# A graph attention layer on one core: the last stage in units of 500 nodes between the last steps, first indices loaded early, target products ten quads behind

## The chip, the cores and the metric

The kernel runs on one core of a Trainium2 chip. The metric is the device time of one execution in microseconds (us). Five engines work side by side, each through its own list of instructions: PE (matrix products), DVE (VectorE), ACT (ScalarE), POOL (GpSimd) and SP (SyncE, which here only issues transfers). Transfers between DRAM and the on-chip memory are issued by SP, ACT or POOL and carried out by 16 DMA engines of the core. An instruction waits on semaphores, and what stands behind it on its engine waits with it.

## The reference, cut to what matters

There are N = 12,500 nodes with 128 channels and E = 400,000 edges, sorted by their target `dst`. The targets are not spread evenly: they are drawn as 12,500 times the square of a uniform number, so many edges go to low nodes.

```python
h = relu(layernorm(x))
message = (h @ w_src + b_src)[src] + (h @ w_dst)[dst]
message = message * edge_weight * radial_mlp(edge_attr)     # three layers, 32-64-64-128
message = message @ w_sep + b_sep                           # 8 heads: 16 alpha, 16 value channels
score = einsum(leaky(alpha), alpha_dot)                     # one for each edge and head
att = segment_softmax(score, dst)
out = x + segment_sum(value * att, dst) @ w_proj + b_proj
```

## The kernel before, in words

**Node stage (L157 to L436).** A loop runs over 25 quads (four tiles of 128 nodes). For quad i it turns and normalizes, makes the source product `products(i, 0)` (L272, stored into the DRAM table `t_src` at L288), and the target product of four quads earlier, `products(i - 4, 1)`, for `t_dst`. After the loop come the last four target products and `cuts()` (L364 to L400), which makes the score vectors on PE (L372) and stores the list `same`, which marks where the target changes. In turn i = 6 `first()` loads the first 128 x 128 source indices `ri` (L295) and turns them into the index tile `idx0` that the first gathers need (L297 to L301). `fits()` (L309) counts sections whose targets span too many nodes into `bad`; if it is not zero, another path runs (it doesn't with these inputs).

**Steps.** The edges form 782 sections of 512, and two sections make a step: NP = 391 steps. `step(k)` (L1219) is a software pipeline written out by hand: in one step it issues loads for later edges (SP: weights, targets, `md` rows of `t_dst` at L844), gathers the source rows for step k + 2 (POOL, L865, an indirect transfer of 128 rows each, 3125 in all), makes messages and scores for steps around k, and LAG = 13 steps later weighs the values and sums them by target in windows of W = 64 nodes: `ob` (L1080). `store_win` (L1084) stores a step's windows into `win`, and `store` (L1087, L1088) writes the 63 first rows of each of the two windows into the DRAM table `agg` (numerator and denominator for each node), at a row number that SP reads from memory. The rows of `agg` are set to zero in the first ten steps by 20 transfers of 125 rows (`zero`, L139). Order and queue of every instruction are those of the program.

**Blocks.** A window's last node can be shared with the next window. Thirteen blocks of 64 sections join these border rows: `block_load`, `block_rows` (loads `rr` from `win`, L1134), `block_maxima`, `block_factors`, `block_columns` (L1163, L1166), `block_totals`, `block_out` into DRAM `obs_d`, and `scatter` (L1195), an indirect transfer on POOL that puts a block's 128 rows into `agg`.

**Drain (L1356 to L1365).** After the last gather, 14 more steps (j = 0 to 13) finish the windows still in the pipeline. In between stand the jobs of the last two blocks, and in steps j = 2 to 12 one load of a finished block's rows (`comb`, L1362) and one scatter. Eight loads on ACT's queue (L1385) bring x + b_proj (`xb`, written earlier) into one tile `x_fin`. A window store into `agg` and a scatter into it are ordered by the program's tracking of dependencies, except in groups that are declared free of each other.

**Last stage (L1390 to L1448).** After the last block's scatter, ten loads bring all of `agg` (`g`, L1399; partition p holds nodes 97p to 97p + 96). Twelve tiles at a time, DVE divides numerator by denominator (L1409 to L1411); for each quad PE turns the quotients (L1422), ACT copies them (L1425), PE multiplies by w_proj (L1433), DVE adds `x_fin` (L1436) and SP stores `out` (L1437).

Of the kernel before, what the change touches and what calls it, by code (L numbers as in the profile page):

```python
# [32 lines left out]
H = 8  # L33
# [23 lines left out]
def gnn_kernel(ctx: ExitStack, tc: tile.TileContext, a: dict, out: bass.AP):  # L57
# [9 lines left out]
    NX = -(-NP // MP) * MP * PR  # L67
    assert NT * P == E and RC * RP == E and NT % TPI == 0 and NT % SORT_T == 0
# [88 lines left out]
    with tc.tile_pool(name="node", bufs=2) as np_, tc.tile_pool(name="node1", bufs=1) as n1, \  # L157
# [22 lines left out]
        ends = n1.tile([NH, 17, 2], I32, name="ends")  # L180
        eb = n1.tile([P, NS, 2], I32, name="eb")
# [6 lines left out]
        def load_targets():  # L188

            nc.sync.dma_start(out=cur[:, 1:CC + 1], in_=dst.rearrange("(p c) -> p c", p=P))  # L190
            at = dst[CC - 1:CC]
            with nc.allow_non_contiguous_dma(reason="single targets"):
                nc.sync.dma_start(out=cur[1:P, 0:1], in_=bass.AP(at.tensor, at.offset, [[CC, P - 1], [1, 1]]))
                at = dst[0:1]
# [97 lines left out]
        def first():  # L292

            ri = n1.tile([P, P], I32, name="ri")
            nc.sync.dma_start(out=ri, in_=src.rearrange("(t p) -> t p", p=P)[0:P, :])  # L295
            rows_0 = n1.tile([P, P], F32, name="rows_0")
            nc.vector.tensor_copy(rows_0, ri)  # L297
            pt = nps.tile([P, P], F32, name="tot", bufs=1)
            nc.tensor.transpose(pt, rows_0, ident)
            nc.vector.tensor_copy(idx0, pt)  # L300
# [8 lines left out]
        def fits():  # L309
# [14 lines left out]
            nc.vector.tensor_copy(bad, sum_)  # L324
# [85 lines left out]
        for i in range(Q):  # L410
# [4 lines left out]
            if i >= 4:  # L415
                products(i - 4, 1)
# [17 lines left out]
        for i in range(Q - 4, Q):  # L434
            products(i, 1)
        cuts()  # L436
# [313 lines left out]
    def windows():  # L750
# [7 lines left out]
        with tc.tile_pool(name="ps", bufs=1, space=PSUM) as pp, \  # L758
# [326 lines left out]

            def store(c, f):
                at = nc.sync.value_load(base[0:1, f, c:c + 1])  # L1087
                st = nc.sync.dma_start(out=agg[ds(at, W - 1), :], in_=accs[c][f * W:(f + 1) * W - 1, :])  # L1088
                if 2 * c + 1 >= (NC - 1) * (P // 2):
                    tc.declare_no_dep(st.ins, group="combined", reason="its rows follow those of the blocks")  # L1090
# [102 lines left out]
            def scatter(g):  # L1193
# [6 lines left out]
                tc.add_to_no_dep_group("combined", st.ins)  # L1200

            comb = {}

            def combined(g):
                comb[g] = tail_pool.tile([P, ROW], F32, name="comb", bufs=2)
                return comb[g]
# [12 lines left out]
            def step(k):  # L1219
# [63 lines left out]
                if has(c - 1):  # L1283
                    sums(c - 1)
                    if k >= NP:
                        store_win(c - 1)
                        store(c - 1, 0)
                        store(c - 1, 1)
# [40 lines left out]

            for k in range(-5, NP):  # L1330
                step(k)
            held.close()


            tail_pool = held.enter_context(tc.tile_pool(name="fin1", bufs=1, side="right"))
            x_fin = tail_pool.tile([P, NB, C], F32, name="x_fin")
            x_loads = load_xb(x_fin)
            last = NC - 1

            def out_rows(g):  # L1340
                block_rows_out(g, combined(g))
                scatter(g)

# [9 lines left out]
                10: lambda: out_rows(last - 1),  # L1353
            }
            assert SB * (NC - 1) + LAG + 1 == NP + 7
            for k in range(NP, NP + LAG + 1):  # L1356
# [9 lines left out]
            for _ in x_loads:  # L1366
                pass
            block_rows(last)
# [4 lines left out]
            with tc.tile_pool(name="fin", bufs=3) as fp:  # L1373
                final(fp, x_fin, lambda i: pp.tile([P, 4, P], F32, name=("pm0", "pm1", "V")[i % 3]),
                      lambda i: pp.tile([P, 4, C], F32, name=("p3", "pa", "m1")[i % 3]))


    XQ = 12
    out_v = out[0:NF * P, :].rearrange("(p t) c -> p t c", t=NF)
    agg_v = agg[0:NF * P, :].rearrange("(p t) c -> p t c", t=NF)  # L1380

    def load_xb(x_fin):

        for t0, t1 in groups:
            nc.scalar.dma_start(out=x_fin[:, t0:t1, :], in_=xb_v[:, t0:t1, :])  # L1385
            yield
        nc.scalar.dma_start(out=x_fin[:tail, NF, :], in_=xb[NF * P:N, :])
        yield

    def final(fp, x_fin, turned, product):  # L1390
        starts = list(range(0, NB, XQ))
        gs, qs, qTs = {}, {}, {}

        def load_g(i):

            gs[i] = fp.tile([P, XQ, ROW], F32, name="g", bufs=len(starts))
            for n, t0, t1 in blocks(starts[i], min(starts[i] + XQ, NB)):
                o = starts[i]
                nc.sync.dma_start(out=gs[i][:n, t0 - o:t1 - o, :],  # L1399
                                  in_=agg_v[:, t0:t1, :] if n == P else agg[NF * P:N, :].unsqueeze(1))  # L1400

        def quotients(i):
            r = fp.tile([P, XQ, H], F32, name="r")
            qs[i] = fp.tile([P, XQ, C], F32, name="q")
            g = gs.pop(i)
            for n, t0, t1 in blocks(starts[i], min(starts[i] + XQ, NB)):
                s = slice(t0 - starts[i], t1 - starts[i])
                m = t1 - t0
                nc.vector.tensor_scalar(r[:n, s, :], g[:n, s, C:ROW], 1e-16, None, op0=ALU.add)  # L1409
                nc.vector.reciprocal(r[:n, s, :], r[:n, s, :])  # L1410
                nc.vector.tensor_mul(  # L1411
                    qs[i][:n, s, :].rearrange("p t (h k) -> p (t h) k", h=H),
                    g[:n, s, 0:C].rearrange("p t (h k) -> p t h k", h=H),
                    r[:n, s, :].unsqueeze(3).to_broadcast([n, m, H, C // H]))

        def turn(i):
            t0, t1 = quads[i]
            q, o = qs[t0 // XQ], t0 // XQ * XQ
            pt = turned(i)
            for t in range(t0, t1):  # L1420
                n = rows(t)
                nc.tensor.transpose(pt[:, t - t0, :n], q[:n, t - o, :], ident[:n, :n])  # L1422
            w = (t1 - t0 - 1) * P + rows(t1 - 1)
            qTs[i] = fp.tile([P, 4, P], F32, name="qT")
            nc.scalar.copy(qTs[i].rearrange("p u n -> p (u n)")[:, :w], pt.rearrange("p u n -> p (u n)")[:, :w])  # L1425

        def finish(i):
            t0, t1 = quads[i]
            qT = qTs.pop(i)
            py = product(i)  # L1430
            for t in range(t0, t1):
                n = rows(t)
                nc.tensor.matmul(py[:n, t - t0, :], qT[:, t - t0, :n], w_proj, start=True, stop=True)  # L1433
            for n, u0, u1 in blocks(t0, t1):
                y = x_fin[:n, u0:u1, :]
                nc.vector.tensor_add(y, py[:n, u0 - t0:u1 - t0, :], y)  # L1436
                nc.sync.dma_start(out=out_v[:, u0:u1, :] if n == P else out[NF * P:N, :].unsqueeze(1), in_=y)  # L1437

        for i in range(len(starts)):
            load_g(i)  # L1440
        quotients(0)
        turn(0)
        for i in range(Q):
            if i % 3 == 1 and i // 3 + 1 < len(starts):
                quotients(i // 3 + 1)
            if i + 1 < Q:
                turn(i + 1)
            finish(i)  # L1448

# [4 lines left out]
    with fit.Else():  # L1454
# [23 lines left out]
        with tc.tile_pool(name="fin_b", bufs=3) as fp, tc.tile_pool(name="fin1_b", bufs=1) as f1, \  # L1478
                tc.tile_pool(name="fin_ps", bufs=2, space=PSUM) as fps, tc.manual_schedule():
            x_fin = f1.tile([P, NB, C], F32, name="x_fin")  # L1480
            for _ in load_xb(x_fin):
                pass
            final(fp, x_fin, lambda i: fps.tile([P, 4, P], F32, name="pt"),
                  lambda i: fps.tile([P, 4, C], F32, name="py"))
# [36 lines left out]
```

## Time and profile before

| | |
|---|---|
| time, median of 3 runs | 4215.05 us (4213.84 to 4223.81) |
| the profiled execution | 4210.53 us, of which the span from first to last instruction is 4208.8 us |
| mean granted clock of PE | 0.977 of full |
| first and last gather start | 82.7 and 4012.2 us |
| PE, DVE, ACT, POOL busy | 93%, 74%, 45%, 72% of the span |
| moved by DMA | 783 MB, 186 GB/s in the mean |

All times within the execution count from the span's start. A row of a timeline gives start and length in us, the engine (a "q" behind it marks an instruction of its sequencer, such as the issue of a transfer), the line, the operation, the tiles as out<-in, and how many instructions were merged; brackets hold the idle time ahead and what ended it. A row of the waits gives who waited for what: us in total, times, longest.

### The profile page before, as it was taken

What the parts mean: (1) busy time and instruction counts of PE and PEld (TensorE: products, weight loads), DVE (VectorE), ACT (ScalarE), POOL (GpSimd) and SP (SyncE); (2) the same over time, 40 slices, a digit from 0 to 9 for tenths busy, and PEclk for the clock granted to TensorE, in tenths of its full rate; (3) what the DMA queues carried; (4) which work ended last, traced back from release to release, by engine and by line L of the source; (5) the groups of instructions that cost most, each with busy time, mean ns of one, the idle gap of its engine ahead of it and who ended that gap; (6) DMA issues with size and microseconds to landing.
All of it is one profiled execution on the core that took longest, in us unless ns stands there. A gap on an engine that the chain in (4) does not pass through costs nothing. (4 is left out here: it accounts for less than half of the span.)

```text
span 4208.8 us, 87885 instructions
## 1 busy us (share of the span) xinstructions
PE 3913.5 (93%) x29351; PEld 2388.5 (57%) x29351; DVE 3104.8 (74%) x6187; ACT 1901.2 (45%) x4549; POOL 3010.2 (72%) x3195
## 2 busy tenths in 40 slices
PE   6889999999999999999999999999999999999975
PEld 5345555555555555555555555555555555555554
DVE  5567777777777777777777777777777777777754
ACT  5344444444444444444444444444444444444421
POOL 4777777777777777777777777777777777777710
PEclk8899999999999999999999999999999999999988
DMA  6767776777776776777777776676677776766634
GB/s 238 235 181 183 187 193 178 197 192 180 198 193 178 197 194 185 189 197 190 184 192 192 181 194 185 177 188 183 178 187 187 185 183 181 189 179 182 184 86 161
DMA packets 593333, 783.08 MB, mean 186 GB/s; under 512 B 125553, under 2 KB 392302, under 8 KB 592740
## 3 DMA queue, kind: packets, MB, share of 16 engines
q1 hardware_dynamic: 384786, 514.16, 40.6%
q0 software_dynamic: 100416, 205.44, 23.9%
q10 hardware_dynamic: 107666, 57.76, 4.7%
q8 instruction: 234, 3.83, 0.4%
q14 instruction: 231, 1.89, 0.1%
HBM read 637.83 MB, written 139.30 MB: 185 GB/s over the span
## 5 line engine op out<-in xcount | busy, mean ns | idle before, releaser
L865 POOL DMA_INDIRECT gs<-t_src,idx x3125 | 2972.3, 951 | 969.2 <-issue 807.5
L954 ACT ACTIVATE sl<-pa,c_b_a 128x512 f32<-128x512 f32 x782 | 536.9, 687 | 1018.6 <-PE pa L952 1009.9
L959 DVE SCALAR_TENSOR_TENSOR al<-pa,sl 128x512 f32<-128x512 f32 x782 | 540.5, 691 | 594.3 <-ACT sl L954 582.9
L1063 PEld LDWEIGHTS V<-c_w_v,mT 128*128 128x128 f32 x6048 | 746.8, 194 | 292.3 <-DVE ob L1080 119.1
L1063 PE MATMUL V<-c_w_v,mT 128*128 128x128 f32 x6048 | 879.4, 289 | 0.0
L952 PE MATMUL pa<-mT,c_w_a 128*128 128x512 f32 x1564 | 814.0, 603 | 3.9 <-DVE mT L946 3.6
L1065 DVE TENSOR_TENSOR pvx<-V,Pem 128x512 f32<-128x512 f32 x756 | 519.2, 687 | 243.4 <-PE V L1063 230.3
L932 PEld LDWEIGHTS pm<-ident,gs 128*128 128x128 f32 x3125 | 393.3, 142 | 420.4 <-issue 289.6
L1076 PEld LDWEIGHTS misc<-pvx,oh 128*64 128x64 f32 x6250 | 352.5, 137 | 410.6 <-ACT h L888 394.3
L924 DVE SCALAR_TENSOR_TENSOR rad<-p,c_fc_b,w_b 128x512 f32<-128x512 f32 x782 | 550.3, 745 | 39.4 <-PE p L916 3.7
L1076 PE MATMUL misc<-pvx,oh 128*64 128x136 f32 x6250 | 453.8, 287 | 118.3 <-ACT h L888 108.3
L946 DVE SCALAR_TENSOR_TENSOR mT<-pm,c_b_src,rad 128x512 f32<-128x512 f32 x782 | 550.7, 746 | 4.8 <-PE pm L939 4.8
L902 ACT ACTIVATE h<-p,b 128x512 f32<-128x512 f32 x391 | 287.5, 735 | 419.8 <-PE p L899 369.1
L932 PE MATMUL pm<-ident,gs 128*128 128x128 f32 x3125 | 471.9, 274 | 0.0
L916 PE MATMUL p<-h,w3b 64*128 64x512 f32 x1564 | 405.4, 595 | 11.5 <-ACT h L902 11.5
L939 PE MATMUL pm<-ohT,m 64*128 64x512 bf16 x2346 | 323.3, 382 | 0.0
L985 ACT ACTIVATE Sp<-m,b_s 128x512 f32<-128x512 f32 x192 | 131.9, 687 | 394.2 <-PE m L968 394.2
L884 PE MATMUL m<-eT,w1b 64*128 64x256 f32 x782 | 274.4, 431 | 26.1 <-DVE M L1006 16.7
L884 PE MATMUL misc<-eT,w1b 64*128 64x256 f32 x782 | 274.4, 431 | 0.0
L1049 DVE TENSOR_TENSOR oh<-lane,misc 128x504 f32<-128x504 f32 x391 | 262.3, 671 | 0.0
L899 PE MATMUL p<-h,w2b 64*64 64x256 f32 x3128 | 259.8, 403 | 0.0
L952 PEld LDWEIGHTS pa<-mT,c_w_a 128*128 128x128 f32 x1564 | 241.9, 195 | 21.2 <-DVE mT L946 8.1
(172 smaller groups left out, 3649.1 us busy)
## 6 DMA issues: line engine op xcount, KB each, us to landing
w_b<-in_edge_weight SPq DMA_DIRECT2D x390, 512.0 KB
d_b<-in_dst SPq DMA_DIRECT2D x390, 256.0 KB
gs<-t_src,idx POOLq DMA_INDIRECT x3125
e_t<-in_edge_attr ACTq DMA_DIRECT2D x390, 128.0 KB
sc_d<-Sp SPq DMA_DIRECT2D x192, 256.0 KB
win<-ob SPq DMA_DIRECT2D x391, 68.0 KB
agg<-ob SPq DMA_DIRECT2D x782, 33.5 KB
md<-t_dst SPq DMA_DIRECT2D x782, 32.0 KB
```

The costliest lines, as they stand in the source:

```text
L865: nc.gpsimd.indirect_dma_start(out=gs[:, t, :], out_offset=None, in_=t_src[:, :], in_offset=bass.IndirectOffsetOnAxis(ap=idx[:, t0 + t:t0 ...
L884: nc.tensor.matmul(p1[q], w1b[s, :], eTs[k][s, :], start=True, stop=True)
L916: nc.tensor.matmul(p3s[k][:, f, 0:SEC], w3b[s, :], h2s[k][s, :], start=True, stop=True)
L924: nc.vector.scalar_tensor_tensor(rad[:, s], p3[:, f, 0:n], b3, w_g[k][:, s], op0=ALU.add, op1=ALU.mult)
L932: nc.tensor.matmul(pms[k, f][:, t * T:(t + 1) * T], gs[:, t, :], ident, start=(t == 0), stop=False, is_transpose=True, skip_group_check=True)
L946: nc.vector.scalar_tensor_tensor(mTs[k][:, s], pms.pop((k, f))[:, 0:n], b_n, rad[:, s], op0=ALU.add, op1=ALU.mult)
L952: nc.tensor.matmul(pa[:, 0:n], w_a, mTs[k][:, f * SEC:f * SEC + n], start=True, stop=True)
L954: nc.scalar.activation(sl[:, 0:n], pa[:, 0:n], AF.Silu, bias=b_a, scale=1.0)
L959: nc.vector.scalar_tensor_tensor(al, pa, 0.25, sl, op0=ALU.mult, op1=ALU.add)
L1063: nc.tensor.matmul(V[:, t, :], mTs[c][:, o:o + T], w_v, start=True, stop=True)
L1065: nc.vector.tensor_mul(pvx[c][:, f, 0:n, 0:C].rearrange("p t (h k) -> p t h k", h=H), V[:, 0:n, :].rearrange("p t (h k) -> p t h k", h=H), ...
L1076: nc.tensor.matmul(acc[f * W:(f + 1) * W, :], ohs[c][:, f * TS + t, :], pvx[c][:, f, t, :], start=(t == 0), stop=(t == n - 1), skip_group_ ...
```

## The change

- `ri` is loaded on SP right behind the first group of x, not in turn 6. Two more single targets (`lim`) are loaded and four small DVE operations add to `bad` whether they are as high as the units below need.
- Target products run ten quads behind the source products instead of four; `cuts()` comes after `products(19, 1)`, so five target products stand behind it.
- The rows of blocks 0 to 10 are brought by four loads in steps NP - 6 to NP - 3, and all eleven scatters are issued at the end of step NP - 3, behind the last gather.
- New groups (`order`) declare that window stores and scatters of different sections are free of each other, and that loads of low nodes need only early sections.
- The last block's rows come in two parts (`last_rows`, `last_rows_2`), the last two of each window straight from the on-chip tile.
- The last stage works in 25 units of 500 nodes, 125 partitions with four nodes each. Seven loads of `g` (ACT's queue) and three of x (SP) are issued in step j = 0; from j = 2 on, `run` finishes one or two units in every step. Units 23 and 24 are loaded on SP after the last scatter.

```diff
         for t0, t1 in groups:
             nc.sync.dma_start(out=x_all[:, t0:t1, :], in_=x_v[:, t0:t1, :])
+            if t0 == 0:
+                ri = n1.tile([P, P], I32, name="ri")
+                nc.sync.dma_start(out=ri, in_=src.rearrange("(t p) -> t p", p=P)[0:P, :])
...
-            if i >= 4:
-                products(i - 4, 1)
+            if i >= 10:
+                products(i - 10, 1)
             products(i, 0)
...
-        for i in range(Q - 4, Q):
+        for i in range(Q - 10, Q):
             products(i, 1)
-        cuts()
+            if i == Q - 6:
+                cuts()
...
                 st = nc.sync.dma_start(out=agg[ds(at, W - 1), :], in_=accs[c][f * W:(f + 1) * W - 1, :])
-                if 2 * c + 1 >= (NC - 1) * (P // 2):
-                    tc.declare_no_dep(st.ins, group="combined", reason="its rows follow those of the blocks")
+                order(st.ins, 2 * c)
...
             for k in range(-5, NP):
                 step(k)
+                if 0 <= k - (NP - 6) < 4:
+                    bring(k - (NP - 6))
+                if k == NP - 3:
+                    for g in range(NC - 2):
+                        scatter(g)
...
-                if 0 <= j - 2 < NC - 2:
-                    nc.sync.dma_start(out=combined(j - 2), in_=obs_d[(j - 2) * P:(j - 1) * P, :])
-                    scatter(j - 2)
-                if j >= 3:
-                    next(x_loads, None)
+                if j == 0:
+                    un.load_x(0, 3)
+                    for u in range(7):
+                        un.load_g(u)
+                if j == 1:
+                    un.quotients(0)
+                    un.quotients(1)
+                    un.turn(0)
+                if j >= 2:
+                    un.run(1 + j % 2, EARLY)
+            un.run(1, EARLY)
             block_columns(last)
+            un.run(1, EARLY)
             block_totals(last)
             out_rows(last)
+            un.run(NU, EARLY)
             work.close()
+            un.run(NU, NU)
...
+    UP, UT = 125, 4
+    UN = UP * UT
...
+        def view(self, t, u):
+            return t[u * UN:(u + 1) * UN, :].rearrange("(p t) c -> p t c", t=UT)
+
+        def load_x(self, u0, u1):
+            for u in range(u0, min(u1, NU)):
+                self.x[u] = self.pool.tile([UP, UT, C], F32, name="xu", bufs=self.nx)
+                nc.sync.dma_start(out=self.x[u], in_=self.view(xb, u))
+
+        def load_g(self, u):
+            self.g[u] = self.pool.tile([UP, UT, ROW], F32, name="g", bufs=self.ng)
+            eng = nc.scalar if u < EARLY else nc.sync
+            self.ng_ = u + 1
+            ld = eng.dma_start(out=self.g[u], in_=self.view(agg, u))
...
+        def finish(self, u):
+            qT, py, y = self.qT.pop(u), self.product(u), self.x.pop(u)
+            for t in range(UT):
+                nc.tensor.matmul(py[:UP, t, :], qT[:, t, :], w_proj, start=True, stop=True)
+            nc.vector.tensor_add(y, py[:UP], y)
+            nc.sync.dma_start(out=self.view(out, u), in_=y)
+            self.nf = u + 1
+
+        def run(self, n, end):
+            for _ in range(n):
+                if self.nf >= end:
+                    return
+                u = self.nf
+                while self.ng_ < min(u + 8, end):
+                    self.load_g(self.ng_)
+                while self.nq < min(u + 3, end):
+                    self.quotients(self.nq)
+                while self.nt < min(u + 2, end):
+                    self.turn(self.nt)
+                self.finish(u)
+                self.load_x(u + 3, u + 4)
```

More of the change, by code (lines that the diff above doesn't have):

```diff
@@ L67, in gnn_kernel @@
     NX = -(-NP // MP) * MP * PR
+    NU = 25
+    EARLY_1, EARLY = 20, 23
+    EARLY_S = [(-(-2 * NS // P) - i) * (P // 2) for i in (2, 1)]
     assert NT * P == E and RC * RP == E and NT % TPI == 0 and NT % SORT_T == 0
@@ L180, in gnn_kernel @@
         ends = n1.tile([NH, 17, 2], I32, name="ends")
+        lim = n1.tile([1, 2], I32, name="lim")
         eb = n1.tile([P, NS, 2], I32, name="eb")
@@ L193, in load_targets @@
                 nc.sync.dma_start(out=cur[1:P, 0:1], in_=bass.AP(at.tensor, at.offset, [[CC, P - 1], [1, 1]]))
+                for i, s in enumerate(EARLY_S):
+                    nc.sync.dma_start(out=lim[:, i:i + 1], in_=dst[s * SEC:s * SEC + 1].unsqueeze(1))
                 at = dst[0:1]
@@ L323, in fits @@
             nc.vector.tensor_reduce(sum_, tot, AX.X, ALU.add)
-            nc.vector.tensor_copy(bad, sum_)
+            low = n1.tile([1, 2], F32, name="low")
+            for i, u in enumerate((EARLY_1, EARLY)):
+                nc.vector.tensor_scalar(low[:, i:i + 1], lim[:, i:i + 1], float(u * (N // NU)), None, op0=ALU.is_lt)
+            nc.vector.tensor_add(sum_, low[:, 0:1], sum_)
+            nc.vector.tensor_add(bad, low[:, 1:2], sum_)
             nc.sync.dma_start(out=ends_d[:, 1:2 * NS + 1].rearrange("o (p c) -> (o p) c", p=NH),
@@ L1084, in store_win, with order @@
                 nc.sync.dma_start(out=win[c * P:(c + 1) * P, :], in_=accs[c])
+            def order(ins, s, whole=False):
+                i = 1 if s < EARLY_S[0] else 2 if s < EARLY_S[1] else 3
+                for j in (1, 2):
+                    if j < i:
+                        tc.declare_no_dep(ins, group=f"early_{j}", reason="its rows follow those of the earlier sections")
+                    if i <= j:
+                        tc.declare_no_dep(ins, group=f"later_{j}", reason="its rows precede those of the later sections")
+                if whole and i < 3:
+                    tc.add_to_no_dep_group(f"early_{i}", ins)
+                if i > 1:
+                    tc.add_to_no_dep_group(f"later_{i - 1}", ins)
             def store(c, f):
@@ L1200, in scatter @@
                 tc.add_to_no_dep_group("combined", st.ins)
+                order(st.ins, g * (P // 2), True)
             comb = {}
-            def combined(g):
-                comb[g] = tail_pool.tile([P, ROW], F32, name="comb", bufs=2)
-                return comb[g]
             stages = {0: lambda g: (block_load(g), block_rows(g)), 2: block_maxima, 4: block_factors,
@@ L1328, in step, with bring, last_rows, last_rows_2 @@
                     stages[o](j)
+            def bring(j):
+                g0, g1 = 3 * j, min(3 * j + 3, NC - 2)
+                t = lp.tile([P, 3, ROW], F32, name="e_t", bufs=4)
+                nc.sync.dma_start(out=t[:, 0:g1 - g0, :],
+                                  in_=obs_d[g0 * P:g1 * P, :].rearrange("(g p) c -> p g c", p=P))
+                for g in range(g0, g1):
+                    comb[g] = t[:, g - g0, :]
+            assert NC - 2 <= 12
             for k in range(-5, NP):
                 step(k)
+                if 0 <= k - (NP - 6) < 4:
[3 more added lines that the diff above has]
+                        scatter(g)
             held.close()
-            tail_pool = held.enter_context(tc.tile_pool(name="fin1", bufs=1, side="right"))
-            x_fin = tail_pool.tile([P, NB, C], F32, name="x_fin")
-            x_loads = load_xb(x_fin)
+            fin = held.enter_context(tc.tile_pool(name="fin", bufs=2, side="right"))
             last = NC - 1
+            un = Units(fin, 8, 9, lambda u: pp.tile([P, 4, P], F32, name=("V", "pa")[u % 2]),
+                       lambda u: pp.tile([P, 4, C], F32, name=("p3", "m1")[u % 2]))
             def out_rows(g):
-                block_rows_out(g, combined(g))
+                comb[g] = fin.tile([P, ROW], F32, name="comb")
+                block_rows_out(g, comb[g])
                 scatter(g)
+            def last_rows():
+                q, s = width(last) // 2, last * (P // 2)
+                rrs[last] = sp.tile([P, ROW], F32, name="rr", bufs=1)
+                for i in range(2):
+                    nc.sync.dma_start(out=rrs[last][i * q:(i + 1) * q - 2, :],
+                                      in_=rows_w[s:s + q - 2, i * (W - 1), :])
+            def last_rows_2():
+                q = width(last) // 2
+                for i in range(2):
+                    nc.sync.dma_start(out=rrs[last][(i + 1) * q - 2:(i + 1) * q, :],
+                                      in_=accs[NP - 1][i * (W - 1):i * (W - 1) + W + 1:W, :])
             jobs = {
@@ L1378, in gnn_kernel @@
[L1378 to L1448, printed above, removed]
@@ new lines, in windows, with __init__, quotients, turn @@
+            un.run(NU, NU)
+    UP, UT = 125, 4
+    UN = UP * UT
+    assert N % UN == 0 and NU == N // UN
+    class Units:
+        def __init__(self, pool, nx, ng, turned, product):
+            self.pool, self.nx, self.ng, self.turned, self.product = pool, nx, ng, turned, product
+            self.x, self.g, self.qT = {}, {}, {}
+            self.nq = self.nt = self.nf = self.ng_ = 0
+        def view(self, t, u):
[9 more added lines that the diff above has]
+            ld = eng.dma_start(out=self.g[u], in_=self.view(agg, u))
+            if u < EARLY_1:
+                tc.declare_no_dep(ld.ins, group="later_1", reason="their nodes follow those of the early units")
+            if u < EARLY:
+                tc.declare_no_dep(ld.ins, group="later_2", reason="their nodes follow those of the early units")
+                tc.add_to_no_dep_group("early_1" if u < EARLY_1 else "early_2", ld.ins)
+        def quotients(self, u):
+            g = self.g[u]
+            r = self.pool.tile([UP, UT, H], F32, name="r")
+            nc.vector.tensor_scalar(r, g[:, :, C:ROW], 1e-16, None, op0=ALU.add)
+            nc.vector.reciprocal(r, r)
+            q = g[:, :, 0:C].rearrange("p t (h k) -> p t h k", h=H)
+            nc.vector.tensor_mul(q, q, r.unsqueeze(3).to_broadcast([UP, UT, H, C // H]))
+            self.nq = u + 1
+        def turn(self, u):
+            g, pt = self.g.pop(u), self.turned(u)
+            for t in range(UT):
+                nc.tensor.transpose(pt[:, t, :UP], g[:, t, 0:C], ident[:UP, :UP])
+            self.qT[u] = self.pool.tile([P, UT, UP], F32, name="qT")
+            nc.scalar.copy(self.qT[u], pt[:, :, :UP])
+            self.nt = u + 1
+        def finish(self, u):
+            qT, py, y = self.qT.pop(u), self.product(u), self.x.pop(u)
+            for t in range(UT):
+                nc.tensor.matmul(py[:UP, t, :], qT[:, t, :], w_proj, start=True, stop=True)
[15 more added lines that the diff above has]
+                self.load_x(u + 3, u + 4)
@@ L1477, in gnn_kernel @@
               ea_s.rearrange("(t p) c -> p t c", p=P), "b")
[L1478 to L1484, printed above, removed]
+        with tc.tile_pool(name="fin_b", bufs=3) as fp, tc.tile_pool(name="fin_ps", bufs=2, space=PSUM) as fps, \
+                tc.manual_schedule():
+            un = Units(fp, 10, 10, lambda u: fps.tile([P, 4, P], F32, name="pt"),
+                       lambda u: fps.tile([P, 4, C], F32, name="py"))
+            un.load_x(0, 3)
+            un.run(NU, NU)
 def kernel(**inputs):
```

14 lines of the change are left out of this document (5 added, 9 removed).

## The prediction, made before the changed kernel was run

> **What bounds the kernel now.** I read the page first (busy shares), then the times of all gathers, then the stretches of 20 us at the end, and last the queues' own waits. Columns of a timeline row: start, length, engine ("SPq" is an instruction that issues or waits), line, operation, tiles, count, and in brackets the idle time before it and what ended it.
>
> ```profile
> PE 3913.5 (93%) x29351; PEld 2388.5 (57%) x29351; DVE 3104.8 (74%) x6187; ACT 1901.2 (45%) x4549; POOL 3010.2 (72%) x3195
> L865 POOL DMA_INDIRECT gs<-t_src,idx x3125: 940/944/2243, 82.7 to 4012.2; - x196
> 82.70:482.70 400.00, 298.95 (x313) 0.91 0.70 192
> 882.70:1282.70 400.00, 302.74 (x320) 0.99 0.73 191
> ```
>
> PE is 93% busy, yet POOL sets the pace: 320 gathers in 400 us are one every 1.25 us, and 3125 of them fill 82.7 to 4012.2 nearly without a hole. An earlier first gather moves the rest with it. What lies outside the gathers is 82.7 us ahead and 4208.8 - 4013 = 196 us behind, and both ends are changed.
>
> The front, in which the change moves a load and six products:
>
> ```profile
> 35.44 0.23 DVE L297 CAST rows<-ri 128x128 f32<-128x128 int32 x1 [7.93 <-DMA ri<-in_src]
> 35.72 0.48 PE L299 MATMUL tot<-ident,rows 128*128 128x128 f32 x1 [8.73 <-DVE rows L297]
> 76.01 6.44 PE L272 MATMUL pm<-w_nodes,x_all 128*128 128x128 f32 x56
> 82.29 0.39 PE L372 MATMUL pt<-c_w_proj,bvb 128*128 128x128 f32 x2
> 98.74 0.27 SPq L398 DMA_DIRECT2D same<-more  x1
> 100.63 1.23 SPq L844 DMA_DIRECT2D md<-t_dst  x2
> ```
>
> DVE and PE stand 8 to 9 us for the first indices; after the products PE makes the score vectors (L372), and only at 98.74 is the last of `same` stored and at 100.63 the first `md` brought, which the first steps need.
>
> The end:
>
> ```profile
> 4040.00:4060.00 20.00, 17.00 (x145) 12.15 (x144) 13.02 (x29) 6.25 (x16) 0.00 (x0) 1.00 0.13 32
> 4060.00:4080.00 20.00, 11.32 (x110) 9.85 (x111) 8.27 (x20) 2.09 (x10) 1.02 (x1) 0.93 0.62 203
> 4140.00:4160.00 20.00, 10.19 (x64) 9.60 (x64) 9.94 (x13) 3.51 (x6) 0.00 (x0) 0.69 0.99 388
> SPq L1088 <- DMA agg<-comb,ids: 20.5, 4, 11.0
> SPq L1088 <- DMA agg<-ob: 12.8, 14, 3.6
> 4126.51 0.30 DVE L1080 TENSOR_TENSOR ob<-misc,bare 128x136 f32<-128x136 f32 x1 [1.10 <-PE misc L1076]
> 4139.32 6.87 SPq L1399 DMA_DIRECT2D g<-agg  x10
> ```
>
> The stretches give busy PE, PEld, DVE, ACT, POOL, PE's clock, the share of the 16 DMA engines and GB/s. In 4040 to 4060 PE works 17 of 20 us. Then the window stores wait for the scatters (20.5 us in four waits between 4050 and 4140), PE falls to 11, and the DMA engines are mostly free. From the last window's sums (4126.51) 12.8 us pass to the loads of `g`; then 128-row loads run at 388 GB/s with all 16 engines busy (0.99), 388 / (0.99 x 16) = 24.5 GB/s for one engine.
>
> **The change, part by part.**
>
> *Front.* With `ri` in SP's line behind the first x group the 8.7 us stall goes. Six more quads of target products stand behind the last source product: 48 matmuls at 6.44 / 56 = 0.115 us, 5.5 us, of which I count 2 to 3, since DVE and ACT must keep the pace too. So the gathers could start about 11 us earlier. But the first steps need `md`, and that stands behind the cuts, `same` and now four more stores of t_dst; it gains the stall less those stores. I take **7 us** off the whole, between 3 and 11. The two loads of `lim` and the four tiny DVE operations lie beside the x loads; cost nothing, at most 1 us.
>
> *Scatters.* Eleven scatters go out in a row after the last gather (POOL is idle there: 0.00 in 4040 to 4060), with their rows brought by four loads in place of eleven. The 20.5 us of waits go. What is late next is not PE but the units, as follows.
>
> *The units.* Each of the 25 units moves 125 rows of 2,048 bytes in (x), 125 of 2,176 in (g) and 125 of 2,048 out: 784,000 bytes, 19.6 MB in all. Before, these transfers had 128 rows. The question is what a transfer of 125 rows gets, and one such stands in the trace: the zeros of `agg`, 125 rows of 2,720 bytes.
>
> ```profile
> agg<-z SPq DMA_DIRECT2D x20, 332.0 KB
> 209.82 3.37 SPq L139 DMA_DIRECT2D agg<-z  x2
> 214.37 0.36 SPq L986 DMA_DIRECT2D sc_d<-Sp  x1
> SPq L991 <- DMA sc_d<-Sp: 9.1, 1, 9.1
> ```
>
> Two of them are issued by 213.2. The 256 KB store of `sc_d` behind them keeps SP waiting 9.1 us (its next issue is at 223.93), while PE, DVE and ACT stand. The DMA view of 218 to 223, inside that wait, in 40 slices of 0.125 us (busy tenths, then GB/s), and its queue rows (q1 is SP's, q0 POOL's gathers):
>
> ```profile
> DMA  3333227872333332993233222279331313338911
> GB/s 131 152 131 131 109 109 229 294 262 87 109 131 147 120 120 103 305 349 131 76 109 131 109 87 87 109 240 311 137 120 71 120 71 120 120 131 213 328 49 33
> q1 hardware_dynamic: 186, 0.45, 23.1%
> q0 software_dynamic: 144, 0.30, 21.5%
> ```
>
> Between the bursts of the gathers (the 7 to 9) the engines are at 0.3, which is 5 of 16, at 109 to 131 GB/s, though the line of zeros is full and eleven engines are free. Queue q1 moves 0.45 MB in 5 us, 90 GB/s on 0.231 x 16 = 3.7 engines: 24.3 for an engine, as above. So a 125-row transfer uses five engines, and successive ones the same five, or the share would be higher. [...]
>
> Five engines at 24.3 are 122 GB/s: **6.4 us for a unit, 160 us for 25**. Bounds: 131 GB/s (6.0 us, 150) and 109 (7.2 us, 180).
>
> When can they start, and what else do the five engines wait for?
>
> ```profile
> 4050.82 0.64 SPq L1126 DMA_DIRECT2D mx<-max_d  x1
> 4052.67 3.21 SPq L1088 DMA_DIRECT2D agg<-ob  x2
> 4057.08 1.75 SPq L1088 DMA_DIRECT2D agg<-ob  x2
> win<-ob SPq DMA_DIRECT2D x391, 68.0 KB
> agg<-ob SPq DMA_DIRECT2D x782, 33.5 KB
> ```
>
> The first loads stand in the program behind the first drain step's block loads, so at about 4051. Compute hides beneath: the drain's next sums come 3.4 us apart when nothing waits (below), and 1.5 units alone are at most 3.6, so 7 us for a step, against 1.5 x 6.4 = 9.6 of transfers. SP issues in order: window, store, wait for its landing, second store, then `out` and x of the unit. While the second store waits for the first (a pair takes 1.75 us), SP feeds nothing, and the pair lands only behind the units' rows on the same engines; only `g` on ACT fills in. I take 1.5 us for each of 13 steps, 20 us (0 if `g` always fills, 3.2 by the slow pair, 42). The window and its stores, 135 KB a step, take another half us each, 7 in all. The last block's 12.8 us chain, which was bare, is hidden: seven units' outputs are still in line. After the last `g` come the last compute, one output and the end, about 8 us (3 + 5, the last from the row below).
>
> ```profile
> 4064.66 0.30 DVE L1080 TENSOR_TENSOR ob<-misc,bare 128x136 f32<-128x136 f32 x1 [0.48 <-PE misc L1076]
> 4068.06 0.30 DVE L1080 TENSOR_TENSOR ob<-misc,bare 128x136 f32<-128x136 f32 x1 [0.42 <-PE misc L1076]
> 4144.09 0.21 DVE L1409 TENSOR_SCALAR r<-g 128x96 f32<-128x96 f32 x1 [8.36 <-issue]
> 4196.87 7.22 SPq L1437 DMA_DIRECT2D out<-x_fin  x6
> ```
>
> (The last output is issued by 4204.1; the span ends at 4208.8. From 4144.1 to 4204.1 the 25 quads take 2.4 us each, a unit's compute at most, for it holds waits too.)
>
> Sum: 4051 + 160 + 20 + 7 + 8 = 4246, less 7 for the front: span **4239** instead of 4208.8. The profiled execution before was 4210.5 with that span, 1.7 outside it, and the median of the three runs, 4215.05, is 4.5 above it. So the forecast is 4239 + 1.7 + 4.5 = **4245 us**, 0.7% slower.
>
> **The rivals.**
>
> *B, all 16 engines (ends faster).* If a 125-row transfer of these is spread as a 128-row one is, a unit takes 784,000 / 388 GB/s = 2.0 us and compute bounds: 4068 + 10 steps x 7 + 12.8 chain + 4.8 for `g` (4139.3 to 4144.1) + 2 x 2.4 + 4.7 = 4165, less 7, span 4158, **4164**. For it: the units' rows are contiguous in DRAM, those of the zeros are not. Against it: on the chip's side both are the same, 125 rows on 125 partitions. The point that decides is the price of a unit: 30 us of loss over 25 units, so at 5.2 us (151 GB/s, six engines) nothing is lost.
>
> *C, five engines, but kept full or relieved (no change).* If `g` on ACT's queue keeps the five busy during each pair (0 in place of 20), or its loads fall on other engines (25 x 2.2 = 56 us beside, most of which compute and stores then take back), the sum is 4239 - 20 to 30: **4215 to 4225**. For it: seven loads of `g` are ahead; nothing in the trace shows ACT's queue with fewer than 16 engines. [...]
>
> *D, the change doesn't do what it says.* If a group of window stores and unit loads still orders one behind the other, no unit starts in the drain. The drain without the scatters' waits would end near 4127 - 20 - 7 = 4100, and 160 + 15 us follow: about **4281**. The groups name each section, which speaks against it.
>
> A front that gains nothing adds 7 to any of them.
>
> **How the numbers follow.** Chances: forecast 0.76, B 0.08, C 0.11, D 0.05. With the ends taken together (150, 0, 11 early: 4211; 180, 42, 3 early: 4291) five engines reach from 4211 to 4291; such ends seldom meet, so the range is 4212 to 4270, which holds most of the forecast and C. A measurement of this kernel tells about 0.3% from no change, 12.6 us: faster is under 4202.4, slower over 4227.7. Slower has D and 0.72 of the forecast, 0.77; the same C and the rest, 0.14; faster B and a shade of C, 0.09.
>
> **What would show it.** In the drain after, the DMA share should sit near 0.3 to 0.4 at 120 to 140 GB/s for some 180 us, PE at a third, SP's waits be for `agg<-ob`, `out` and x, DVE's for `g` and x; sums of windows 10 to 13 us apart. A share near 0.9 in bursts, or sums 6 to 7 us apart, proves B. The first gather should come near 72. If the drain's sums run at 3.4 us with no units between, it is D.

## The result, and the profile after

The changed kernel takes **4268.1 us** (median of 4 runs, 4266.3 to 4272.9), the kernel before 4216.3 us in the same comparison: ratio 1.0121, with a 95% interval of 1.0108 to 1.0133. It is 52 us slower: inside the range of 4212 to 4270, but only 2 us below its upper end and 23 above the forecast of 4245. The profiled execution has a span of 4267.7 us.

First the gathers of the changed kernel, from the view of their tile, and then the stretch from the first to the last unit (busy PE, PEld, DVE, ACT, POOL, PE's clock, share of the 16 DMA engines, GB/s):

```profile
L877 POOL DMA_INDIRECT gs<-t_src,idx x3125: 938/945/2892, 75.0 to 4010.4; - x196
```

```profile
4050.00:4250.00 200.00, 92.16 (x652) 82.59 (x650) 73.89 (x178) 20.60 (x59) 1.88 (x2) 0.70 0.32 105
```

The first gather starts 7.7 us earlier than before, the last one 1.8 us earlier. What counts stands behind them: from the end of the last gather to the end of the span (below, **the tail**) it was 4208.8 - 4013.2 = 195.6 us before and is 256.1 now. For 200 us of it the DMA engines are 0.32 busy, 5.1 of 16, and move 105 GB/s, while PE, the busiest of the five engines, works 92 of 200 us.

The same in slices of 20 us, and SP's waits from 4040 to the end:

```profile
4070.00:4090.00 20.00, 17.03 (x147) 15.49 (x144) 15.44 (x36) 4.88 (x16) 0.00 (x0) 0.90 0.30 93
4090.00:4110.00 20.00, 14.99 (x129) 13.23 (x128) 8.74 (x20) 2.10 (x7) 0.00 (x0) 0.91 0.33 118
4110.00:4130.00 20.00, 7.69 (x48) 7.30 (x48) 7.99 (x25) 1.73 (x6) 0.00 (x0) 0.57 0.30 97
...
4230.00:4250.00 20.00, 2.98 (x22) 2.75 (x20) 2.07 (x3) 0.58 (x1) 0.00 (x0) 0.67 0.33 127
4250.00:4267.00 17.00, 5.15 (x24) 4.59 (x24) 3.83 (x8) 1.15 (x2) 0.00 (x0) 0.60 0.15 44
```

```profile
SPq L1112 <- DMA agg<-ob: 82.2, 16, 10.7
SPq L1485 <- DVE xu L1484: 27.7, 6, 15.7
```

From 4070 to 4250 every slice lies between 0.28 and 0.34: that is what five engines look like in this view. The mean alone would not say so, for the kernel before has 0.35 and 108 GB/s from 4050 to 4140; but its slices of 20 us there go from 0.18 to 0.62. The waits for scatters (20.5 us before) are gone, and 82.2 us of waits for the stores' own landing, which were 12.8, stand in their place.

The chain of work that ended last (start, length, what it stood for) shows which waits count. Three of its longest pieces:

```profile
4146.23 12.86 DMA agg<-ob
4227.06 12.18 DMA xu<-xb
4240.85 12.56 DMA g<-agg
```

From 4040 to the end, 33.3% of this chain is the landing of window stores, 17.0% that of x and 9.9% that of `g`. So the units reach the critical path mostly through SP's line: the second window store waits until the first has landed, which has units' rows ahead of it, and SP issues nothing meanwhile. With 128 rows (e10 below, 4040 to 4166, the share of the engines up to 0.71 in a slice of 20 us) the same three are 4.8, 2.4 and 5.9%, and PE leads.

How the window sums move, from the timelines of DVE (the last step's of before stands in the prediction at 4126.51):

```profile
4049.25 0.30 DVE L1092 TENSOR_TENSOR ob<-misc,bare 128x136 f32<-128x136 f32 x1 [0.40 <-PE misc L1088]
4071.24 0.30 DVE L1092 TENSOR_TENSOR ob<-misc,bare 128x136 f32<-128x136 f32 x1 [0.86 <-PE misc L1088]
...
4185.50 0.29 DVE L1092 TENSOR_TENSOR ob<-misc,bare 128x136 f32<-128x136 f32 x1
4194.88 0.29 DVE L1092 TENSOR_TENSOR ob<-misc,bare 128x136 f32<-128x136 f32 x1
```

At 4049 both kernels are at the same step (before: 4049.45). From there to the last sums it takes 146 us instead of 77, and from the last sums to the end 73 instead of 82.

### The profile page after: what moved, and what is told of

Same layout as the page of the kernel before. It is cut to its first block, busy times and chain, and to the rows that moved or that the text cites. A ratio compares the mean times of both kernels' runs of the same rounds, so it can differ in the third digit from the quotient of the medians.

```text
span 4267.7 us, 87970 instructions
## 1 busy us (share of the span) xinstructions
PE 3928.6 (92%) x29357; PEld 2400.2 (56%) x29357; DVE 3110.1 (73%) x6234; ACT 1902.2 (45%) x4549; POOL 3011.8 (71%) x3195
## 4 chain that ended last, share of the span: by engine, by line
PE 80%; DMA 7%; DVE 5%; ACT 4%; issue 2%; SPq 2%; ACTq 0%; DVEq 0%; POOL 0%
PE V L1075 17%; PE pa L964 14%; PE misc L1088 9%; PE pm L944 7%; PE p L928 7%; PE pm L951 7%; PE m L896 5%; PE p L911 5%; PE m L980 5%; DMA agg<-ob 2%; PE m L887 2%; DVE M L1023 1%; ACT L966 1%; DMA w_b<-in_edge_weight 1%; DMA xu<-xb 1%
## 6 DMA issues: line engine op xcount, KB each, us to landing
d_b<-in_dst SPq DMA_DIRECT2D x390, 256.0 KB
sc_d<-Sp SPq DMA_DIRECT2D x192, 256.0 KB
```

## The experiments

**Theory 1**: a transfer of 125 rows is carried by five of the 16 engines, always the same, and the 75 transfers of the units set the pace on those five. **Theory 2**: SP's line of issues, with the window stores' waits in it, sets the pace, and the engines are idle because of it. A third question is what the front and the scatters give by themselves.

The first four runs were made on a chip on which the kernel before takes 5312 us, where the gathers come more slowly. A stretch of 400 us of e3 shows it:

```profile
1000.00:1400.00 400.00, 327.97 (x2319) 194.46 (x2320) 244.44 (x490) 148.18 (x357) 243.73 (x255) 0.96 0.54 149
```

It holds 255 gathers, where a stretch as long of before holds 320. The expectations were written with 4215 in mind; what is compared is the difference to before on the same chip, and the tail. The later runs were made on two chips where the kernel before takes 4217 us (e5 to e8) and 4214 us (e9 to e11). Two kernels ran on the slow chip and on one of these, and their tails are 10 and 12 us longer on the slow one (184 and 174 us, 168 and 156 us). So tails of different chips can be compared to some 12 us only.

### e1 and e2: each transfer cut in two, at row 112 and at row 115

```diff
+    PARTS = [(0, 112), (112, UP)]
...
-                nc.sync.dma_start(out=self.x[u], in_=self.view(xb, u))
+                for p0, p1 in PARTS:
+                    nc.sync.dma_start(out=self.x[u][p0:p1], in_=self.view(xb, u)[p0:p1])
```

(The loads of g and the outputs likewise; in e2, 115 stands in place of 112.)

> The changed kernel with every transfer of a unit issued as two, rows 0 to 111 and rows 112 to 124; the queues, the order and the work are the same. [...] Theory 2 (SP's line of issues, with the window stores' waits of 82 us, sets the pace whatever the engines do): twice as many issues in that line, 4265 to 4300 us.

> [...] Theory 2: the same as the cut at 112, within 10 us. If a smaller transfer by itself were better, this one would fall as well.

Measured: the cut at 112 is 14 us faster than before (ratio 0.9968, 0.9944 to 0.9992), its tail 184 us. The cut at 115 is 56 us slower (1.0091, 1.0062 to 1.0120), its tail 256.0 us, as long as that of the changed kernel. (That they agree to 0.1 us is chance, since the chips differ.) Both cuts have the same issues in the same order. The stretch of 200 us in the tail of the cut at 115:

```profile
5145.00:5345.00 200.00, 101.19 (x672) 90.40 (x671) 77.46 (x185) 21.77 (x61) 1.88 (x2) 0.68 0.34 106
```

0.34 and 106 GB/s again. So it is not the number of issues that decides between the two, nor that a transfer was cut, but the row at which it is cut: a part of 115 rows fares as the whole of 125 does (tails of 256.0 and 256.1 us), a part of 112 doesn't (184). What makes 112 and 115 differ, no run shows. Theory 2 is out as a cause by itself: twice the issues in the same line are faster when the cut is at 112. SP's waits are then one way in which the few engines cost time. The gain of the cut at 112 fell short of the 30 us and more that I had estimated; it is taken up again in e9.

### e3: units of 512 nodes on 128 partitions

```diff
-    UP, UT = 125, 4
-    UN = UP * UT
+    UT = 4
+    UN = P * UT
+
+    def up(u):
+        return (min(N, (u + 1) * UN) - u * UN) // UT
```

(The last unit has 212 nodes on 53 partitions, cut at 48; low nodes are 19 and 23 units.)

> The changed kernel with 24 units of 512 nodes (128 partitions with four nodes each) and a last one of 212 nodes, one transfer each as before the cut; low nodes are 19 and 23 units. Theory 1: 16 engines, 2.0 to 2.2 us a unit, and DVE, PE and the stores bound the drain: 4155 to 4180 us, a little under the cut at 112 because there are fewer issues. Theory 2: 4255 to 4275 us, since the line on SP is the same.

Measured: 43 us faster than before (0.9908, 0.9879 to 0.9938), tail 168 us. The row count of 128 in place of 125 turns a loss into a gain, with the line on SP as it was but for the bounds of the units.

### e4: the scatters' part alone

```diff
-                if 0 <= j - 2 < NC - 2:
-                    nc.sync.dma_start(out=combined(j - 2), in_=obs_d[(j - 2) * P:(j - 1) * P, :])
-                    scatter(j - 2)
...
+                if k == NP - 3:
+                    for g in range(NC - 2):
+                        scatter(g)
```

> The kernel before with the scatters' part of the change alone: blocks 0 to 10 brought by four loads and scattered behind the last gather, window stores and scatters declared free of each other by sections; last stage and front as before. Theory 1: the waits of 20.5 us of stores for scatters go and the drain ends some 20 us earlier, then the ten loads of all of g and the last stage follow as before: 4190 to 4200 us. Theory 2 (the stores' own waits set the drain): within 10 us of before.

Measured: 6.5 us faster by the medians, while the ratio of 0.9971 (0.9955 to 0.9986) stands for 15 us (7 to 24); on this chip the gain is not known better than that. The tail is 188 us. That is 8 less than before's, which is from another chip, so it doesn't settle the size either. I expected 20 us. SP's waits in its drain show what is left:

```profile
SPq L1101 <- DMA agg<-ob: 18.7, 16, 4.9
SPq L1423 <- DMA agg<-comb,ids: 5.5, 1, 5.5
```

The waits for scatters are gone but for the last, yet the stores wait for one another 18.7 us (12.8 before), with the loads of `x_fin` beside them. How much of the expected 20 us is missing, and what of it falls to those waits and what to PE, was not separated.

### e5: the front alone

```diff
-            if i >= 4:
-                products(i - 4, 1)
+            if i >= 10:
+                products(i - 10, 1)
...
+            if i == Q - 6:
+                cuts()
```

(And `ri` behind the first x group.)

> The kernel before with the front of the change alone: the first indices loaded behind the first x group, target products ten quads behind, the cuts after the twentieth target product; drain and last stage as before. The prediction's step: the first gather some 8 to 11 us earlier, and 7 us (3 to 11) off the whole. Rival, from the trace of the changed kernel (first gather 7.7 us earlier, last one 1.8): what is gained ahead is lost again along the gathers, and the time is within 3 us of before.

Measured: 4210.0 against 4217.2 us, 7.2 us faster (0.9981, 0.9972 to 0.9990). The gathers of its profile:

```profile
L867 POOL DMA_INDIRECT gs<-t_src,idx x3125: 939/945/2764, 73.2 to 4007.6; - x196
```

The first is 9.5 us earlier, the last 4.6. The rival read a loss of 6 us along the gathers out of one execution of the changed kernel (last gather 4010.4). In this profile, too, 4.9 of the 9.5 us are gone at the last gather. But the profiled execution of before lies 4.5 us under its median, so a loss read against it need not be the change's, and the medians gain 7.2. The profiles of the other runs with this front on a chip like it start their last gather between 4007.4 and 4010.4, so it varies from one execution to the next by some 3 us, and a single profile can't price a term of this size.

### e6: the cut at 100

```diff
-    PARTS = [(0, 112), (112, UP)]
+    PARTS = [(0, 100), (100, UP)]
```

> The changed kernel with every transfer of a unit issued as two, rows 0 to 99 and 100 to 124: as many issues as in the runs cut at 112 and at 115. [...] Theory 2 (SP's line of issues): the same as one of the others, without an order by engines.

Measured: 4208.2 against 4217.2 us, 9 us faster (0.9981, 0.9971 to 0.9990), tail 199 us; I expected a tail of 210 to 225 and a loss of 10 to 30 us, which rested on an estimate of mine that the cut at 100 costs 0.6 of the whole transfer; so the price is below that or is hidden in part. The order is the expected one: tails of 256, 199 and 174 to 184 us for the cuts at 115, 100 and 112. How many engines a part of 100 or of 25 rows gets was not shown.

### e7 and e8: the first loads of g and the first quotients a step later

```diff
                 if j == 0:
                     un.load_x(0, 3)
-                    for u in range(7):
+                    for u in range(2):
                         un.load_g(u)
                 if j == 1:
-                    un.quotients(0)
-                    un.quotients(1)
-                    un.turn(0)
+                    for u in range(2, 7):
+                        un.load_g(u)
```

In the changed kernel the second drain step loses 16 us. The timeline shows why:

```profile
4046.62 7.76 ACTq L1456 DMA_DIRECT2D g<-agg  x7
4056.04 1.22 DVE L1018 TENSOR_TENSOR_SCAN M<-m,S 128x512 f32<-128x512 f32 x1 [5.02 <-DMA g<-agg]
4065.07 0.48 DVE L1170 TENSOR_TENSOR_SCAN up<-cuts,up,mx 128x128 f32<-128x128 bf16 x1 [2.86 <-DMA mx<-max_d]
4066.85 1.09 PE L1475 MATMUL V<-ident,g 125*128 125x125 f32 x4 [16.24 <-DVE g L1469]
```

Seven loads of `g` are queued, the small loads of the last softmax and block land behind them, DVE waits for these, and the quotients stand behind on DVE; PE has the first turn in front of its next step and waits 16.2 us. It looks like a cause.

> The changed kernel, still with 125 rows, but two loads of g in step j = 0 and five in j = 1, and the first quotients in step j = 2 instead of j = 1, so that the small loads of the last softmax no longer stand behind seven loads of g and PE doesn't wait 16 us for the first quotients. Theory 1 (five engines have 180 us of work): the wait moves, it doesn't go: within 8 us of the changed kernel, 45 to 60 us slower than before. Rival (the 16 us of the second drain step are lost for good): 30 to 40 us slower than before.

> The run with units of 512 nodes, with the loads of g and the first quotients moved in the same way. Theory 1: with 16 engines the drain is bound by PE and DVE, so a wait that goes there is a gain: 3 to 8 us faster than the units of 512 alone, which were 43 us faster than before; so 45 to 52 us faster than before.

Measured: with 125 rows (e7) 4268.8 against 4217.2 us, ratio 1.0125 (1.0110 to 1.0141): nothing gained. The last window sums stand at 4193.5, where they were at 4194.9:

```profile
4063.90 0.29 DVE L1092 TENSOR_TENSOR ob<-misc,bare 128x136 f32<-128x136 f32 x1
...
4193.53 0.29 DVE L1092 TENSOR_TENSOR ob<-misc,bare 128x136 f32<-128x136 f32 x1
```

```profile
4050.00:4250.00 200.00, 93.80 (x635) 83.78 (x630) 73.20 (x176) 20.35 (x57) 2.20 (x2) 0.67 0.32 104
```

The wait went elsewhere, as theory 1 has it: where the units' transfers on five engines set the length of the drain, PE's 16 us of waiting are a symptom. With 128 rows (e8) 4171.2 against 4217.2 us, 46 us faster; that this is more than without the later loads is not borne out by e10.

### e9 and e10: the cut at 112 and the units of 512 nodes on a chip like the first

> The cut at 112 once more, to stand beside the cut at 100 on a chip where the kernel before takes 4217 us. [...]

> Units of 512 nodes alone, to stand beside the same with later loads of g (46 us faster than before). Expected 3 to 8 us slower than that: 38 to 43 us faster than before. If the 16 engines take the whole collision of the first loads away by themselves, no difference.

Measured, against 4213.5 us: the cut at 112 gives 4186.0 us, 27.5 faster (0.9936, 0.9920 to 0.9953), tail 174; the units of 512 give **4168.9 us, 44.6 faster** (0.9899, 0.9882 to 0.9915), tail 156. With 128 rows the collision of the first loads costs nothing that later loads would save: 44.6 and 46 us, each against before on its own chip, are the same within their intervals. The stretch of 100 us, first of the cuts at 100, then at 112, then of the units of 512:

```profile
4050.00:4150.00 100.00, 69.12 (x562) 62.48 (x563) 61.88 (x147) 16.57 (x51) 0.97 (x1) 0.83 0.48 142
```

```profile
4050.00:4150.00 100.00, 71.72 (x599) 64.84 (x599) 66.66 (x160) 18.31 (x54) 0.97 (x1) 0.87 0.58 161
```

```profile
4050.00:4150.00 100.00, 77.54 (x648) 70.54 (x648) 73.36 (x175) 20.59 (x57) 1.88 (x2) 0.88 0.61 191
```

From 0.32 over 0.48 and 0.58 to 0.61, and 105, 142, 161, 191 GB/s: the drain follows the share and the rate until PE and DVE, at 78 and 73 of 100, come near to bounding it. SP's waits for the window stores go the same way, from 82.2 us over 25.7 to 13.1 and 18.3, with the same stores. In the units of 512 nodes the last window sums stand at 4127.2, less than 1 us behind those of before (4126.51), with most of the last stage already done beside them. The cut at 112 reaches a share of 0.66 in a slice of 20 us (10.6 of 16) and loses 17 us to the units of 512, which reach 0.71; it issues 75 transfers more on two queues, which fits, but no run separates it.

### e11: x and the outputs of the units on POOL's queue

```diff
-                nc.sync.dma_start(out=self.x[u], in_=self.view(xb, u))
+                nc.gpsimd.dma_start(out=self.x[u], in_=self.view(xb, u))
...
-            nc.sync.dma_start(out=self.view(out, u), in_=y)
+            nc.gpsimd.dma_start(out=self.view(out, u), in_=y)
```

> The changed kernel, 125 rows in one transfer as there, but x and the outputs of the units are issued by POOL, which is idle in the drain; g stays on ACT. If the number of engines follows from the rows whatever the queue, and they are the same five: 50 us slower than before, as the changed kernel. If POOL's transfers of 125 rows go to other or to all engines, only g's 55 us stay on the five, and the drain falls to about that of the cut at 112 or 100: 0 to 30 us faster than before. SP's line is relieved in both cases, so theory 2 expects a gain as well; the DMA share in the drain tells the two apart (0.3, or more).

Measured: 4205.0 against 4213.5 us, 8.6 faster (0.9981, 0.9971 to 0.9990), tail 194. Slices of its drain:

```profile
4090.00:4110.00 20.00, 10.33 (x96) 9.53 (x95) 7.86 (x21) 1.62 (x6) 3.03 (x6) 0.81 0.38 122
4110.00:4130.00 20.00, 15.01 (x107) 13.50 (x106) 12.92 (x35) 3.41 (x11) 3.28 (x7) 0.76 0.62 181
4130.00:4150.00 20.00, 18.20 (x175) 16.68 (x175) 17.71 (x42) 4.42 (x13) 7.05 (x13) 1.00 0.67 199
```

With whole transfers of 125 rows, some 60 us come back by the queue alone, and the share reaches 0.67, so POOL's transfers aren't kept to the five engines that SP's and ACT's use. 0.67 is 10.7 of 16; how many engines a single one of them takes, and which, the trace doesn't show. SP's line is relieved as well (its waits for window stores fall from 82.2 to 43.6 us), and how much of the 60 us comes from that was not separated.

## Why the prediction was right or wrong, point by point

- **Five engines, the same for all transfers of SP and ACT: right.** 0.32 of 16 for 200 us, the tails of some 256 us of the changed kernel, e2 and e7, and the order of e2, e6, e1/e9 and e3/e10. The share and the distance of the window sums (12 us in the mean) are as the prediction named them; the rate (105 GB/s, not 120 to 140) and PE's share (0.46, not a third) are not. That `g` on ACT's queue falls on the same five, for which no row of before spoke, is borne out by the share as well: SP and ACT together don't exceed it (0.34 at most in the slices of 20 us from 4070 on). For the other cuts the runs give shares of 0.48 (at 100) and 0.58 (at 112) in the mean of 100 us; no run shows how many engines one part gets there, nor what sets the number.
- **The units' price: the term that was mis-sized.** The prediction set 160 us for transfers, 20 for the waits of store pairs and 7 for the windows, 187 us for 19.6 + 1.75 MB, 114 GB/s. Measured were 105 GB/s over 200 us on 5.1 engines: 20.5 GB/s for an engine, not the 24.3 of the zeros or the 24.5 of the large loads. 21.35 MB at 105 GB/s are 203 us, 16 more. But 20.5 is a mean of unlike stretches, as the DMA view of two windows of 5 us shows (40 slices of 0.125 us each, then SP's queue), first 4230 to 4235, then 4115 to 4120:

```profile
DMA  3233323233324223332333333323233323233233
q1 hardware_dynamic: 316, 0.62, 32.2%
DMA  0000016200000000034444347212760020642005
q1 hardware_dynamic: 414, 0.19, 23.6%
```

  In the first, x loads and outputs follow one another with no window rows between them, and an engine moves 0.62 MB / 5 us / (0.322 x 16) = 24 GB/s, as forecast; so it is not the two directions by themselves that cost. In the second, the engines first stand, since SP has waited for a window store until 4115.3; then they are busy, but at 10 GB/s for an engine. Of the 1,600 slices of 0.125 us from 4050 to 4250, 186 are under a tenth busy, 23 us, about the 20 that the prediction set for the waits; the rest of the 16 us must then lie in stretches like the end of the second window. What slows the rows there stays open; no run measured it alone.
- **The end: 8 us for the last compute, output and close, too little.** The last loads of `g` go out behind all other outputs, and little else is left for the DMA engines while the chain runs (0.15 from 4250 on):

```profile
4240.42 2.18 SPq L1456 DMA_DIRECT2D g<-agg  x2
4251.27 0.18 DVE L1466 TENSOR_SCALAR r<-g 125x32 f32<-125x32 f32 x1 [11.24 <-DMA g<-agg]
4258.36 1.55 SPq L1485 DMA_DIRECT2D out<-xu  x2
```

  From 4240.4 to 4267.7 are 27 us, of which two loads of `g` and two outputs are 8.7 by the prediction's rate: 18.6 without, not 8. With the 16 of the rate that makes the 26 us by which the stage took longer (first load 4046.6 to 4267.7, 221 us, against the prediction's 4044 to 4239, 195).
- **The front, 7 us: right** (7.2 in e5), with the first gather 7.7 to 9.5 us earlier instead of 11. In the profiled execution of the changed kernel only 1.8 of it was left at the last gather; the first loads of the units went out at 4046.6 instead of 4044, which is the remaining 2.7 us of the span. The 4.5 us that I put between the profiled execution and the median were not there this time (4267.7 + 1.7 against 4268.1). So the span was missed by 29 us and the time by 23: that the time stayed inside the range owes something to these 4.5 us, which is luck.
- **The scatters: the waits went, and what is late next was named rightly** (the units and the stores behind them); e4, without the units, shows the stores alone as the next wait, and a gain of 6.5 us by the medians.
- **The last block's chain hidden beneath the outputs: right**: behind the last window sums the changed kernel needs 73 us, and outputs of the waiting units run from 4196 to 4240.
- **B, 16 engines: its mechanism isn't this kernel's, but its price was close**: 4164 forecast for it, 4168.9 and 4171.2 measured once the rows are 128. In part that is the same luck: its span of 4158 stands against 4166.0 in e10. **C**: the five were not kept full (23 us under a tenth busy) and not relieved. **D**: window stores and unit loads don't order each other; the first loads go out at 4046.6.

## What to carry to other kernels

Before cutting a transfer into new pieces, look at the number of rows that it gets, not only at its bytes: with 125 rows this change costs 52 us where with 128 it gains 45, with the same bytes and queues. A low mean of the DMA share can be idleness or few engines, and here the drains of both kernels are near it (0.35 before, 0.32 after); the slices of 20 us tell them apart: with few engines the share stayed between 0.28 and 0.34 here, with waits it went from 0.18 to 0.62. And a long wait in front of one instruction (16 us of PE here) can be worth nothing when something else sets the length of the stretch: move it and measure before believing it.

## What the runs showed of the hardware that was not expected

- Cutting one transfer of 125 rows into 112 and 13 shortens the tail from 256 to 174 us, though it doubles the issues; cutting it at 115 leaves it at 256 us.
- The queue matters for transfers of such a row count: the same 125 rows from POOL's queue bring the share from 0.32 to as much as 0.67 in a slice of 20 us.
- One chip ran the kernel before, and two variants of the changed one that also ran elsewhere, some 1100 us slower, nearly all of it along the gathers (0.54 of DMA share, 255 gathers in 400 us in place of 320); the tails of the two variants were only 10 and 12 us longer there. Why its gathers are slower was not looked into.
